# Second pair's Gram matrices ahead of the first merging, its inversion and solution inside the first pair's work, and a reordered opening

## The chip, the cores and the metric

The kernel runs on one core of a Trainium2 chip. The metric is the device time of one execution in microseconds; the time shown is the median of several executions. All times below come from these executions and from one profiled execution with its trace. The engines are TensorE (PE for its matmuls, PEld for its weight loads), VectorE (DVE), ScalarE (ACT), GpSimd (POOL) and SyncE (SP), which issues most DMAs.

## What is computed

For 32 sequences of 512 rows and 256 features: a delta-rule block with an MLP, both on normalized rows, then a gated MLP with integer weights, each added to its input.

```python
def delta(x, ...):
    q, k, v = jnp.split(x @ gates_w + gates_b, 3, axis=-1)
    lr = x @ lr_w + lr_b
    k = k / jnp.linalg.norm(k, axis=-1, keepdims=True)
    K = jnp.tril(jnp.einsum('ntc,nsc->nts', k, k), k=-1)
    u = solve_triangular(K + jnp.eye(T), v, lower=True)
    score = jnp.einsum('nsk,ntk->nst', q, k)
    y = jnp.einsum('nst,ntv->nsv', score, lr * u)
    return y @ out_w + out_b

def attn(x, ...):
    x = x + delta(layernorm(x, dn_g, dn_b), ...)
    return x + relu(layernorm(x, mn_g, mn_b) @ w1 + b1) @ w2 + b2

def ffn(x, ...):                     # wg, wu, wd = integers / 127
    return (silu(x @ wg.T) * (x @ wu.T)) @ wd.T

x = x + attn(_layernorm(x), ...)
x = x + ffn(_layernorm(x), ...)
```

## The kernel before

The 32 sequences are worked through in 16 pairs. A sequence is four chunks of 128 rows (NT = 4), its features two blocks of 128 (NF = 2). Everything is 32-bit float, and each product of 128 by 128 by some columns appears as two MATMUL records. The order of the work is written out by hand for every engine: each engine runs its instructions in program order, and the order of the Python calls is that order. Tiles come from rings of buffers by tag ("hid", "fz", "uv", "ps_a", "ps_f"), and a new tile waits for the last reader of the one whose place it takes.

A sequence goes through these steps:

- `normalized`: statistics on VectorE (L409, L410), centring with a sum on ScalarE (L527), scaling on VectorE (L543). `to_keys` turns it by TensorE for the first two pairs (tp_a, L465), later pairs by DMA (way_a, ag).
- `keys` (pk, L588) and `gram` (pg, L617): the Gram matrix in four block rows, copied by ScalarE into gd (diagonal blocks), go (blocks off the diagonal) and, in `give`, gs. `give` also sends the 32x32 diagonal blocks by eight DMAs a pair (given, L635) to DRAM.
- `invert` (L656 on): the blocks come back by one DMA (blocks, L661), and VectorE inverts the 128 small triangles of a pair in 15 steps of a product and a sum (xt, L710 and L716). The result goes out and back by DMA (found, yb, yfull). It is a generator that can run as a `Side`: `spend(cols)`, called after matmuls, lets it advance by so much weight per column. `norms` makes the factors kn.
- `solution`: `merge` joins the small inverses to 128x128 (xparts, pw, py, yfull; L750 to L798) in five steps, `solve` runs the block solution (pr, pu, rhs, dp) in eight more.
- values: `gather` (pf), `through_values` (pz), `through_keys` (pm), `answer` (po_d, then statistics m).
- first MLP (`middle`): `normed`, `turned`, `mlp_in` (pa), `mlp_out` (po_m), `residual`; then the gated MLP (`gated`, 84 steps, L1007) and its output `Down` (po_x, po_y), which runs beside the next pair's values.

In a regular pair the next pair's preparation, keys and Grams run within the gated MLP, its inversion within the values, and its merging and solution from `middle` into the gated MLP. In the first pair this starts up: gate weights are folded with the norm's gains (`Gates.fold`, wlast, wt, pbias), products lT and rv are made (`Gates.rest`), the first pair is inverted with nothing beside it but the second pair's keys and the turning of the integer weights (wd_t, wg_t, wu_t), and then merged and solved. The second pair's Grams stand between the first pair's values and answers (`first_values`), its inversion is a side of the first MLP and of the first gated MLP up to step BEGIN = 17, its merging begins after step 21.

Of the kernel before, what the change touches and what calls it, by code (L numbers as in the profile page):

```python
# [10 lines left out]
F32 = mybir.dt.float32  # L11
# [5 lines left out]
B = 32  # L17
# [5 lines left out]
def kernel(  # L23
# [46 lines left out]
    INVERT = 17 * 1024  # L70
    INVERT_FIRST = 15 * 1024

# [117 lines left out]
    nc.gpsimd.memset(sel[:, LAST:P], 1.0)  # L190

    class Gates:


        def __init__(self, gw):

            self.gw = gw
            self.gb = wk.tile([1, GC], F32, tag="feat", name="gb", bufs=4)
            self.wlast = wk.tile([P, GC], F32, tag="feat", name="wlast", bufs=4)
            self.wt = [wk.tile([P, GC], F32, tag="dp", name=f"wt{f}") for f in range(NF)]  # L200
            self.load(*CUTS[0], nc.scalar)
            self.dnb = by_feature(dn_b, "dnb", nc.sync)
            self.dng = by_feature(dn_g, "dng", nc.sync)
            self.glast = const.tile([P, 1], F32, name="glast")
            nc.sync.dma_start(self.glast, dn_g[C - 1 : C].partition_broadcast(P))
            self.put = wk.tile([P, NF, P], F32, tag="rhs", name="put", bufs=4)
            nc.gpsimd.memset(self.put, 0.0)
            nc.gpsimd.tensor_copy(self.put[:, :, LAST:P], self.dnb.unsqueeze(2))
# [18 lines left out]

        def fold(self, lo_, hi_):

            cut = slice(lo_, hi_)  # L230
            pb = ps_f.tile([P, 512], F32, tag="mm", name=f"pbias_{lo_}")
            pb = pb[:, : hi_ - lo_]
            for f in range(NF):
                nc.tensor.matmul(
                    pb, lhsT=self.put[:, f, :], rhs=self.gw[f][:, cut],
                    start=(f == 0), stop=False,
                )
            nc.tensor.matmul(pb, lhsT=sel, rhs=self.gb[:, cut], start=False, stop=True)
            nc.vector.tensor_scalar(
                self.wlast[:, cut], self.wlast[:, cut], self.glast, None, ALU.mult  # L240
            )
            for f in range(NF):
                nc.vector.scalar_tensor_tensor(
                    out=self.wt[f][:, cut], in0=self.gw[f][:, cut],
                    scalar=self.dng[:, f : f + 1], in1=self.wlast[:, cut],
                    op0=ALU.mult, op1=ALU.subtract,
                )
            nc.vector.tensor_tensor(
                self.wt[NF - 1][:, cut], self.wt[NF - 1][:, cut], pb, ALU.add
            )  # L250

        def keys(self):
            self.fold(*CUTS[0])
            for f in range(NF):
# [27 lines left out]

        def rest(self):
            nc.vector.tensor_scalar(obrow, self.obs, ident[:, LAST:P], None, ALU.mult)
            self.fold(*CUTS[1])
            self.fold(*CUTS[2])
            kT_ = self.turned(C, "wkT")
            qT_ = self.turned(0, "wqT")
            vT_ = self.turned(2 * C, "wvT")
            self.product(lT, kT_, qT_, "lT")  # L290
            self.product(rv, vT_, self.ow, "rv")

            ones = wk.tile([P, P], F32, tag="wl", name="ones", bufs=1)
# [10 lines left out]
            nc.scalar.copy(wl, pl)  # L304

        def load_rest(self):
            self.load(*CUTS[1], nc.sync)
            self.load(*CUTS[2], nc.sync)
            self.room = wk.tile([P, NH, NF, C], F32, tag="hid", name="room")
            self.rooms = 0  # L310
            self.ow = self.scratch("ow")
# [73 lines left out]
    class Combined:  # L385


        def __init__(self):
            self.b12 = wk.tile([P, NP, P], F32, tag="fz", name="b12", bufs=4)

# [191 lines left out]
    def keys(s, o):  # L582
        n = s.n
        if o == 0:
            s.kT = wk.tile([P, NF, T], F32, tag="ka", name=f"kT_{n}")
        pk = ps_a.tile([P, 512], F32, tag="mm", name=f"pk_{n}_{o}")
        for f in range(NF):
# [19 lines left out]
    def gram(s, j):  # L607
# [3 lines left out]
        if j == 0:  # L611
            s.gd = wk.tile([P, NT, P], F32, tag="gd", name=f"gd_{n}", bufs=2)
            s.go = {}
        w = (NT - j) * P
        pg = ps_a.tile([P, 512], F32, tag="mm", name=f"pg_{n}_{j}")
        for f in range(NF):
# [5 lines left out]
        if j < NT - 1:  # L622
            s.go[j] = wk.tile([P, w - P], F32, tag=f"go{j}", name=f"go_{n}_{j}", bufs=2)
            nc.scalar.copy(s.go[j], pg[:, P:w])
        spend(NF * w)

    def give(s, given):

        s.gs = wk.tile([P, NT, 2, B], F32, tag="gs", name=f"gs_{s.n}")
        second = s.gd.rearrange("p b (a h r) -> p b a h r", h=2, r=B)[:, :, :, 1, :]  # L630
# [26 lines left out]
    def invert(g, given, seqs):  # L657

        blocks = wk.tile([P, B, B], F32, tag="blocks", name=f"blocks_{g}", bufs=1)
        n, nq, ncol = len(seqs), columns.nq, columns.nc  # L660
        nc.sync.dma_start(  # L661
            blocks,
            given.rearrange("s b i e -> (s b i) e")[:, : B * B].unsqueeze(1).to_broadcast(
                [n * NT * NB, nq, B * B]
            ),
        )
        flat = blocks.rearrange("p i j -> p (i j)")
# [223 lines left out]

    def answer(s):
        pr = Project(ps_f, s.a, s.aT, s.m, NF, f"d{s.n}", s.r2[:, 0, :])
        s.norm = Norm(s.a, f"m{s.n}")
        for c in range(NT):
            pr.step(c)
            if c % 2 == 1:
                s.norm.measure(c - 1)
# [332 lines left out]

    whole = lambda gen: [None for _ in gen]

    def middle(old, rest, sides_, sol, following):
# [40 lines left out]
        if not rest:  # L1275
            next(sides_[0].gen)
            sides_[0].finish()

    def last_middle(old, rest):
        one, two = old  # L1280
# [20 lines left out]

    def first_values(seqs, following, norms_, inverse, given):

        one, two = seqs
        for _ in normalized(following[1]):
            pass
        gates.rest()
        for _ in inverse:
# [22 lines left out]
        for turn in turns[:2]:  # L1331
            for _ in turn:
                pass
        turns = turns[2]
        for s in seqs:
            for _ in rates(s):
                pass
        for _ in solution(seqs):
            next(turns, None)
        for _ in turns:  # L1340
            pass
        whole(gather(one))
        whole(gather(two))
        gram(following[0], 0)
        fetch_residual(one)
        biased(one)
        whole(through_values(one))
        gram(following[0], 1)
        fetch_residual(two)
        biased(two)  # L1350
        whole(through_values(two))
        gram(following[0], 2)
        whole(through_keys(one))
        gram(following[0], 3)
        give(following[0], given[0])
        answer(one)
        whole(through_keys(two))
        normed(one, "m")
        answer(two)
        gram(following[1], 0)  # L1360
        turned(one, "m")
        gram(following[1], 1)
        gram(following[1], 2)
        gram(following[1], 3)
        give(following[1], given[1])
        for s in following:
            for _ in rates(s):
                pass
        return sides_of(begun(following, given), INVERT_FIRST)

# [67 lines left out]
    with tc.manual_schedule(engines={  # L1438
# [5 lines left out]
        gw = [wk.tile([P, GC], F32, tag="a", name=f"gw{f}", bufs=6) for f in range(NF)]  # L1444
        size = NH * C
        places = [
            wk.tile([P, 2, size], I32, tag="hid", name="integers"),
# [9 lines left out]
        ]  # L1457
        load_a(first[0])
        gates = Gates(gw)
        load_a(first[1])  # L1460
# [9 lines left out]
        mnb = by_feature(mn_b, "mnb", nc.sync)  # L1470
        for _ in normalized(first[0]):
            pass
        to_keys(first[0])
        gates.keys()
        for _ in normalized(first[1]):
            pass
        given = new_given(0)
        for i, s in enumerate(first):
            if i:
                to_keys(s)  # L1480
                for _ in normalized(pairs[1][0]):
                    pass
            for o in range(NF):
                keys(s, o)
            in_order(s)
            grams(s)
            give(s, given[i])
        norms_, inverse = begun(first, given)
        for d, _ in quantized:
# [3 lines left out]
        for g in range(n_pairs):  # L1493
            new = pairs[g]
            following = pairs[g + 1] if g + 1 < n_pairs else None
            if not old:
                given = new_given(1)
                sides_ = first_values(new, following, norms_, inverse, given)
                rest = []
            else:  # L1500
                sol = solution(new)
                middle(old, rest, sides_, sol, following)
                prep = None
# [10 lines left out]
                for i, _ in enumerate(gated(old)):  # L1514
                    if i >= EARLY and i % 2 == 0 and solved:
                        next(early, lambda: None)()
                    if i == BEGIN and not rest:
                        sides_[1].finish()
                    if i % 3 == 2 and (rest or i >= BEGIN + 4):
                        solved = next(sol, sol) is sol  # L1520
# [72 lines left out]
```

## Time and profile before

| quantity | us |
|---|---|
| median of three executions (2070.45 to 2075.43) | 2072.32 |
| the profiled execution | 2069.12 |
| its span in the trace | 2067.3 |
| TensorE busy | 1992.1 (96%) |
| VectorE busy | 1370.9 (66%) |
| GpSimd busy | 1113.9 (54%) |
| ScalarE busy | 918.1 (44%) |
| first inversion on VectorE | 43.93 to 64.12 |
| first merging (pw) starts | 69.90 |
| first gather starts | 92.97 |
| second pair's inversion on VectorE | 134.09 to 166.7 |
| second merging (pw) starts | 172.15 |
| second pair's gather starts | 229.18 |

In lines of the trace the columns are: start and length in us, engine, line, operation, output and inputs by the program's names, shape, count, and in brackets the engine's idle time before it with what ended it. A granted clock (PEclk) of 1.00 is TensorE's full speed. A wait line reads: engine, waiting tile and line, what it waited for: us in total, times, longest.

### The profile page before, as it was taken

How to read it: one execution, taken by the hardware profiler on the slowest of the kernel's cores; microseconds unless marked ns; L12 is line 12 of the kernel's file. 1: busy time of each engine (PE TensorE's matmuls, PEld its weight loads, DVE VectorE, ACT ScalarE, POOL GpSimd, SP SyncE). 2: the span in 40 equal slices, each digit the busy share in tenths (PEclk: the TensorE clock that was granted, in tenths of full speed). 3: DMA queues.
4: the chain of work that ended last, by engine and by line, in shares of the span. 5: the costliest groups of instructions: out<-in, count | busy, mean ns of one | idle time of the engine just before them, and what ended most of it. 6: DMA issues, size and time to landing. Idle time of an engine off the chain costs nothing.

```text
span 2067.3 us, 31099 instructions
## 1 busy us (share of the span) xinstructions
PE 1992.1 (96%) x10286; PEld 1583.0 (77%) x10286; DVE 1370.9 (66%) x3788; ACT 918.1 (44%) x2499; POOL 1113.9 (54%) x1317
## 2 busy tenths in 40 slices
PE   6888999999999999999999999999999999999998
PEld 4657876878778687886878778687877878778887
DVE  5567584966848587584966848587585867848252
ACT  4235345353543535345353543535345353544443
POOL 3424464645546465454645536475455646536668
PEclk9899999999999999999999999999999999999999
DMA  5111242332323323142332323233242332423120
GB/s 146 28 34 29 53 132 58 90 99 60 105 63 100 83 71 112 50 134 57 90 102 61 106 62 100 83 76 107 58 126 64 94 90 61 113 54 100 42 62 21
DMA packets 248344, 164.12 MB, mean 79 GB/s; under 512 B 80849, under 2 KB 223832, under 8 KB 248184
## 3 DMA queue, kind: packets, MB, share of 16 engines
q1 hardware_dynamic: 247670, 161.61, 28.8%
q8 instruction: 82, 1.34, 0.3%
q14 instruction: 78, 0.64, 0.1%
q10 hardware_dynamic: 434, 0.39, 0.1%
q0 software_dynamic: 80, 0.14, 0.0%
HBM read 96.02 MB, written 66.06 MB: 78 GB/s over the span
## 4 chain that ended last, share of the span: by engine, by line
PE 72%; DVE 16%; DMA 6%; ACT 2%; issue 2%; POOL 1%; SPq 1%; POOLq 0%; DVEq 0%; ACTq 0%
PE po_y L1134 6%; PE pg L617 6%; PE pyup L1007 5%; PE pk L588 5%; PE pygate L1007 5%; PE pa L951 5%; PE po_m L876 5%; PE po_d L876 4%; PE pr L814 4%; PE po_x L1134 4%; PE pzup L1007 4%; PE pf L835 4%; PE pzgate L1007 4%; DMA ag<-way_a 3%; PE pu L824 3%
## 5 line engine op out<-in xcount | busy, mean ns | idle before, releaser
L1047 POOL TENSOR_TENSOR v_up<-v_up,five_up 128x256 f32<-128x256 f32 x96 | 70.0, 729 | 266.5 <-ACT v_up L1021 266.5
L1070 DVE TENSOR_TENSOR top_up<-top_up,pzup 128x512 f32<-128x512 f32 x96 | 65.5, 682 | 218.2 <-PE pzup L1007 215.7
L1134 PEld LDWEIGHTS po_y<-wdS,hid 128*128 128x128 f32 x1536 | 179.7, 192 | 4.1 <-issue 1.0
L1134 PE MATMUL po_y<-wdS,hid 128*128 128x128 f32 x1536 | 182.8, 276 | 0.0
L1007 PE MATMUL pygate<-hS,wgS 128*128 128x256 f32 x576 | 175.0, 386 | 4.6 <-ACT top_gate L1041 2.3
L1007 PE MATMUL pyup<-hS,wuS 128*128 128x256 f32 x576 | 174.5, 385 | 1.9
L617 PE MATMUL pg<-kT 128*128 128x256 f32 (+3 forms) x512 | 157.6, 433 | 1.9 <-ACT kT L595 1.9
L1134 PEld LDWEIGHTS po_x<-wdS,hid 128*128 128x128 f32 x1152 | 138.4, 192 | 5.1 <-POOL hid L1071 1.9
L1134 PE MATMUL po_x<-wdS,hid 128*128 128x128 f32 x1152 | 138.9, 275 | 1.7 <-POOL hid L1071 1.7
L1053 POOL TENSOR_TENSOR hid<-v_gate,five_gate 128x256 f32<-128x256 f32 x96 | 69.7, 726 | 130.7 <-ACT v_gate L1021 130.7
L1075 DVE TENSOR_TENSOR hid<-top_gate,pzgate 128x512 f32<-128x512 f32 x96 | 65.1, 678 | 112.4 <-PE pzgate L1007 112.4
L1007 PEld LDWEIGHTS pyup<-hS,wuS 128*128 128x128 f32 x576 | 106.2, 190 | 43.1 <-issue 13.4
L1007 PEld LDWEIGHTS pygate<-hS,wgS 128*128 128x128 f32 x576 | 106.4, 190 | 41.7 <-issue 12.4
L588 PE MATMUL pk<-ag,wa 128*128 128x512 f32 x256 | 122.5, 603 | 13.6 <-DMA ag<-way_a 12.5
L1048 POOL TENSOR_TENSOR hid<-hid,v_up 128x256 f32<-128x256 f32 x96 | 70.3, 733 | 102.9 <-ACT hid L1054 93.1
L876 PE MATMUL po_m<-w2s,act 128*128 128x256 f32 x512 | 125.4, 389 | 0.1
L1071 POOL TENSOR_TENSOR hid<-hid,top_up 128x512 f32<-128x512 f32 x96 | 122.4, 1275 | 0.3 <-DVE bnst_a L409 0.3
L617 PEld LDWEIGHTS pg<-kT 128*128 128x128 f32 x512 | 92.0, 190 | 37.1 <-issue 9.3
L1007 PE MATMUL pzup<-hT_f,wuS 128*128 128x256 f32 x384 | 117.9, 389 | 1.2 <-ACT five_up L1021 0.7
L951 PE MATMUL pa<-hT_m,w1s 128*128 128x512 f32 x256 | 116.7, 598 | 1.9 <-DMA hT_m<-way_m 1.9
L835 PE MATMUL pf<-a,dp 128*128 128x256 f32 x512 | 115.4, 379 | 0.0
L1007 PE MATMUL pzgate<-hT_f,wgS 128*128 128x256 f32 x384 | 115.2, 382 | 0.1
(242 smaller groups left out, 4905.4 us busy)
## 6 DMA issues: line engine op xcount, KB each, us to landing
a<-in_L_attn_x_dram SPq DMA_DIRECT2D x32, 512.0 KB, 4.7
x<-in_L_attn_x_dram SPq DMA_DIRECT2D x32, 512.0 KB, 4.3
out_dram<-a SPq DMA_DIRECT2D x64, 256.0 KB, 2.8
way_m<-turn_m SPq DMA_DIRECT2D x120, 128.0 KB, 2.4
hT_m<-way_m SPq DMA_DIRECT2D x30, 512.0 KB, 4.0
way_a<-turn_a SPq DMA_DIRECT2D x112, 128.0 KB, 2.3
ag<-way_a SPq DMA_DIRECT2D x28, 512.0 KB, 3.6
way_f<-turn_f SPq DMA_DIRECT2D x112, 128.0 KB, 2.3
```

The costliest lines, as they stand in the source:

```text
L588: nc.tensor.matmul(pk, lhsT=wa[:, f, ts(o, P)], rhs=s.ag[:, f, :], start=(f == 0), stop=(f == NF - 1),)
L617: nc.tensor.matmul(pg[:, :w], lhsT=s.kT[:, f, ts(j, P)], rhs=s.kT[:, f, j * P :], start=(f == 0), stop=(f == NF - 1),)
L814: nc.tensor.matmul(pr, lhsT=s.go[j][:, ts(i - j - 1, P)], rhs=p_[:, j, :], start=(j == 0), stop=(j == i - 1),)
L835: nc.tensor.matmul(s.pp[:, o, :], lhsT=lhs[:, c, ts(o, P)], rhs=rhs[:, c, :], start=(c == 0), stop=(c == nk - 1),)
L876: nc.tensor.matmul(self.po[:, c % 2, :], lhsT=src[:, ts(c, P)], rhs=self.w[:, f, :], start=(f == 0), stop=(f == self.nk - 1),)
L951: nc.tensor.matmul(pa, lhsT=w1s[:, f, ts(o, P)], rhs=s.hT[:, f, :], start=(f == 0), stop=(f == NF - 1),)
L1007: nc.tensor.matmul(dst, lhsT=self.w[:, self.j, self.SLOT[i], :], rhs=self.s.B[i], start=first, stop=last, skip_group_check=True,)
L1047: nc.gpsimd.tensor_tensor(v, v, self.five, ALU.add)
L1048: later(5, lambda: nc.gpsimd.tensor_tensor(self.out(1, 1), self.out(1, 1), self.half(v), ALU.mult))
L1053: nc.gpsimd.tensor_tensor(to, self.half(v), self.half(self.five), ALU.add)
L1071: later(4, lambda: nc.gpsimd.tensor_tensor(natural(g), natural(g), grouped(flat(self.top)), ALU.mult))
L1134: nc.tensor.matmul(po[:, i, :], lhsT=self.A[block][:, j, :], rhs=wdS[:, j, slot, :], start=(j == 0), stop=(j == NP - 1),)
```

## The change

Five things are done. The gains of the gate weights are split from `fold` and made earlier (`gains`), `bias` and `shift` stay; the preparation of the later sequences is cut into pieces between keys and Grams. The first pair's blocks are loaded in two halves, one a sequence. The second pair's keys and Grams use ps_f, and the Grams of both sequences lie in one tile of tag "hid", filled ahead of the first merging. Its inversion becomes a side of the first pair's values (weight spread over 17 x 1024 columns instead of 15 x 1024). A `first_middle` takes its merging in, and the first gated MLP goes on with the solution from its third step.

```diff
-    INVERT_FIRST = 15 * 1024
+    INVERT_FIRST = 17 * 1024
...
-        def keys(self):
-            self.fold(*CUTS[0])
+        def shift(self, to, pb):
+            nc.vector.tensor_tensor(to, to, pb, ALU.add)
+
+        def keys(self, between):
+            folded = self.fold(*CUTS[0])
+            between()
+            self.shift(*folded)
...
-        def rest(self):
-            nc.vector.tensor_scalar(obrow, self.obs, ident[:, LAST:P], None, ALU.mult)
-            self.fold(*CUTS[1])
-            self.fold(*CUTS[2])
+        def rest(self, prep):
+            for folded in [self.bias(*cut) for cut in CUTS[1:]]:
+                self.shift(*folded)
...
+            whole(prep)
...
+        def gains(self):
+            for cut in CUTS[1:]:
+                self.gain(*cut)
+            nc.vector.tensor_scalar(obrow, self.obs, ident[:, LAST:P], None, ALU.mult)
...
-            self.b12 = wk.tile([P, NP, P], F32, tag="fz", name="b12", bufs=4)
+            self.b12 = wk.tile([P, NP, P], F32, tag="uv", name="b12", bufs=1)
...
-        pk = ps_a.tile([P, 512], F32, tag="mm", name=f"pk_{n}_{o}")
+        pk = (ps_f if n // NS == 1 else ps_a).tile([P, 512], F32, tag="mm", name=f"pk_{n}_{o}")
...
+            if n // NS == 1:
+
+                if n % NS == 0:
+                    pairs[1][1].some = s.some = wk.tile(
+                        [P, NS, NT * (NT + 3) // 2 * P - T // 2], F32, tag="hid", name="grams",
+                    )
...
+        parts = n if g == 0 else 1
+        for q in range(parts):
+            rows = slice(q * (n // parts), (q + 1) * (n // parts))
+            nc.sync.dma_start(
+                blocks[q * (P // parts) : (q + 1) * (P // parts)],
...
+    def first_middle(old, newer, sides_, sol, following):
+        one, two = old
+        step = lambda: next(sol, None)
+        normed(two, "m")
+        mlp_in(one, 0)
+        mlp_in(one, 1)
+        turned(two, "m")
+        sides_[1].finish()
+        next(sides_[0].gen)
+        sides_[0].finish()
+        residual(one)
+        for s in newer:
+            whole(rates(s))
+        mlp_out(one, 0)
+        mlp_out(one, 1)
+        residual(two)
+        mlp_in(two, 0)
+        step()
+        mlp_in(two, 1)
+        normed(one, "f")
+        step()
+        mlp_out(two, 0, step)
+        turned(one, "f")
+        step()
+        whole(mixed(one))
+        mlp_out(two, 1, step)
+        load_a(following[0])
...
+        for s, m in zip(following, given):
+            grams(s)
+            give(s, m)
+        gens = begun(following, given)
         for s in seqs:
-            for _ in rates(s):
-                pass
+            whole(rates(s))
         for _ in solution(seqs):
-            next(turns, None)
+            next(turns[2], None)
+        whole(turns[2])
+        sides_ = sides_of(gens, INVERT_FIRST)
+        next(gens[1])
         whole(gather(one))
-        whole(gather(two))
-        gram(following[0], 0)
+        other = gather(two)
+        next(other)
         fetch_residual(one)
         biased(one)
         whole(through_values(one))
+        whole(other)
+        whole(through_keys(one))
         fetch_residual(two)
         biased(two)
         whole(through_values(two))
-        gram(following[0], 2)
...
+        answer(one, lambda: whole(through_keys(two)))
         normed(one, "m")
         answer(two)
-        gram(following[1], 0)
         turned(one, "m")
...
+        prep = normalized(first[1])
+        gates.keys(lambda: some(prep, NT - 1))
+        some(prep, 2)
         given = new_given(0)
+        some(prep, 2)
+        keys(first[0], 0)
+        some(prep, 1)
+        keys(first[0], 1)
+        some(prep, 1)
+        in_order(first[0])
+        grams(first[0])
+        give(first[0], given[0])
+        inverse = invert(first[0].n, given, first)
+        next(inverse)
+        whole(prep)
+        to_keys(first[1])
+        prep = normalized(pairs[1][0])
+        some(prep, NT + 3)
+        gates.gains()
+        last = normalized(pairs[1][1])
+        some(last, NT + 1)
+        keys(first[1], 0)
...
-                    if i == BEGIN and not rest:
-                        sides_[1].finish()
-                    if i % 3 == 2 and (rest or i >= BEGIN + 4):
+                    if i % 3 == 2:
                         solved = next(sol, sol) is sol
```

## The prediction

> **What bounds the kernel now.** I read first the page's 40 slices, then a cut of the span into stages at the points that the change touches, then TensorE's waits up to 230 us, then TensorE and VectorE in order of time through those stages.
>
> ```profile
> PE   6888999999999999999999999999999999999998
> PEclk9899999999999999999999999999999999999999
> ```
>
> From the sixth slice on TensorE is full at full clock. A change to the opening can only win in the first five slices, and can only lose where it disturbs the rest. The stages (columns: start:end, length, busy us and instructions of PE, PEld, DVE, ACT, POOL, granted clock, DMA share, GB/s) are: opening up to the first merging, merging and solving of the first pair, its values, its first MLP with the second pair's inversion, its gated MLP with the second pair's solution, one regular pair, all others.
>
> ```profile
> 10.99:69.90 58.91, 47.94 (x182) 29.30 (x182) 44.33 (x147) 28.09 (x89) 26.38 (x19) 0.93 0.38 102
> 69.90:92.97 23.07, 21.73 (x112) 16.98 (x113) 9.79 (x21) 4.47 (x14) 5.69 (x9) 0.65 0.00 1
> 92.97:124.45 31.48, 30.95 (x137) 24.37 (x136) 11.72 (x48) 9.86 (x26) 7.96 (x10) 1.00 0.14 36
> 124.45:150.26 25.81, 19.97 (x67) 12.49 (x65) 16.27 (x49) 10.39 (x24) 5.84 (x7) 0.88 0.24 65
> 150.26:229.18 78.92, 70.96 (x330) 54.29 (x328) 46.35 (x125) 40.39 (x115) 29.64 (x36) 0.95 0.13 33
> 229.18:354.72 125.54, 122.23 (x634) 96.79 (x633) 84.18 (x227) 56.29 (x157) 65.83 (x79) 1.00 0.32 85
> ```
>
> TensorE idles 58.91-47.94 = 10.97, then 1.34, 0.53, 5.84 and 7.96 us: 26.6 us. The missing clock is worth 0.07x58.91 + 0.35x23.07 + 0.12x25.81 + 0.05x78.92 = 4.1+8.1+3.1+3.9 = 19.2 us. So 46 us is the ceiling. Who ended the waits:
>
> ```profile
> PE pw L756 <- DVE xparts L751: 7.8, 2, 4.5
> PE tp_f L465 <- ACT turn_f L446: 4.5, 1, 4.5
> PE pygate L1007 <- ACT top_gate L1041: 2.3, 1, 2.3
> PE pwqT L267 <- DVE wt L243: 2.3, 1, 2.3
> PE pg L617 <- ACT kT L595: 1.9, 1, 1.9
> PE pygate L1007 <- DVE hid L1075: 1.2, 1, 1.2
> ```
>
> Both mergings wait for the inversion behind xparts (4.50 and 3.29 us), and after each such gap the clock is halved. The same sixteen pw take 1.97 us at 69.90 and 1.15 in the next pair:
>
> ```profile
> 69.90 1.97 PE L756 MATMUL pw<-xparts,gs 128*64 128x64 f32 x16 [4.50 <-DVE xparts L751]
> 271.33 1.15 PE L756 MATMUL pw<-xparts,gs 128*64 128x64 f32 x16
> ```
>
> **The change part by part**, stage by stage against the profiled execution's own times.
>
> **Opening (58.91).** ScalarE's four centrings (x8, 2.07 us) no longer stand as a block ahead of the two kT copies: of pg's 1.91 us and the later overlaps I take 2.05. The gains (0.35+0.88 for one cut, 0.35+0.89 for the other, obrow 0.35: 2.8 us of VectorE) and the last sequence's statistics (some 2.5) move into VectorE's waits of 4.03 us at 29.4 and 3.66 at 37.8. The folds then end with their bias matmuls, and the waits 2.30+0.53+0.45 = 3.28 before pwqT and pwvT go; with them the half clock of 42 to 48 us (pwqT, plT 3.62 against 1.89 for eight matmuls of the same shape, prv) is worth 2.5. The second pair's 32 Gram matmuls come here: 1.72+1.29+0.86+0.43 = 4.3 us a sequence, 8.6 for both; they stand where the 4.50 wait was. VectorE then decides: spread ends near 39.3, the inversion (43.93 to 64.12, 20.2 us) starts there, ends at 59.9, and b1s, w1s (2.2), eight rates (2.75) and two transposes (0.9) bring the first pw to 65.75; TensorE, by its own rows, reaches it at 65.4. The blocks must be there by 39.5: the second half's load now waits only for the second sequence's givens; the split adds one DMA of about 0.6 us on SP, which is waiting for givens anyway, and without that cover costs 0.6. So the opening takes 54.8: **-4.1** net of the 8.6.
>
> The bound: if VectorE's order is worse by the whole 2.05, 0; if the block load is the limit (38.44 issue to 43.93 at most in the trace, only 1.4 us earlier now), 2.8 later.
>
> **Merging and solving (23.07).** No work changes; the clock does. pw, py, pw, py took 1.97, 1.92, 1.97, 1.94 against 1.15, 1.12, 1.14, 1.14: 3.25; two pu blocks 2.07+1.82 against 1.03 each: 1.83; pr 1.91 against 1.03: 0.88. **-5.9**. TensorE would be some 74% busy in the merging; the slices of 2 us with 1.28 and then 0.41 busy (152 to 156) kept clock 1.00, so I let it stay.
>
> **Values (31.48).** The Gram matrices leave (8.7 with their overlaps) and an m wait of 0.46: 22.3. Here the inversion comes in, with its blocks and ss DMAs ahead of the x loads on SP (SP is free near 71, the x loads are due near 86). 17,408 columns for its weight let its 15 steps run through to the last answer. VectorE gets 20.2 us of inversion and 8.5 of answers (four halves of 0.88+0.74+0.30, two m of 0.42) beside 20.8 us of TensorE, and is late. Placed step by step, the first answer's statistics end some 22.35 us after the stage's start, r_m and mr_m (1.04+0.20 and gaps) at 23.7, ScalarE's chunks 24.3 to 25.8; TensorE is ready for tp_m at 20.8. A new wait of 3.5 us plus a paced tp_m, 4.3 together: 26.6, **-4.9**.
>
> **First MLP (25.81).** Gone: 0.90+0.16 before tp_m, 4.51 before tp_f, 3.0 of half clock. In: four merging blocks of 1.08 (4.3), and two waits for ScalarE, whose turn_m of the second sequence now stands ahead of the relus and waits for statistics that end behind the inversion's last step (28.95): 1.4+0.9 = 2.3. And the clock: a 3.5 us gap is like the 3.29 and 4.50 that were followed by half speed; 3 us (the half clock priced in this stage now), counted at 0.8: 2.4. Sum -8.6+9.0, say **0**. If VectorE keeps up, 9 us better; if its lag is double, about 6.6 more wait here and in the values, and with another cold stretch (3) 10 worse.
>
> The yb round trip (xc copied at 166.66, transposed at 171.21) hides behind mlp_out of the first sequence. The rates (2.75 us of VectorE) stand after residual in the first MLP; the first sequence's output waits for them, inside the 2.3.
>
> **Gated MLP (78.92).** Merging leaves (-4.3), the waits 3.29, 1.24, 0.69, 0.34 go, 1.3 of the 2.31 goes (turn_f of the second sequence is less late), half clock at 172 to 178 (pw 0.82, pzup, pygate, pyup 1.6, py 0.5) -3.0; a wait of 1.2 for ag, as at 326.88 in the next pair, comes. **-12.9**. The solution ends near step 26 of 84; the second hid takes the Gram tile's place and is first written past step 42, 16 steps or 7 us later. Without that cover the hid copies would wait for the last pr.
>
> The smaller buffers (b12 in uv, keys and Grams in four ps_f banks instead of ps_a's three) cost nothing: ScalarE empties a Gram in 0.75 us while the first two take 1.72 and 1.29.
>
> **Sum:** -4.1-5.9-4.9+0-12.9 = -27.8. Own time 2069.12 (span 2067.3 and 1.8 around it) gives 2041.3; the median 2072.32 lies 3.2 above, and I predict **2044** for the median.
>
> **Rivals.**
>
> *VectorE becomes the bound of the values and the first MLP.* For it: between gather and the gated MLP VectorE has 20.2+8.5, residuals 2.4, rates 2.75, four halves of mlp_out 6.6 and some 3 of merging, 43 us, against 44 of TensorE. Against: only tp_m, m and mlp_out wait for it. Price 10 over mine: about 2054.
>
> *VectorE keeps up.* For it: steady pairs run inversion and values together with waits of 0.7 (po_d on m). Against: they have Down work beside it. 9 us better: 2035.
>
> *The two sequences' Grams in one tile are held as one.* Then ScalarE's copies for the second wait until the first's given DMAs, behind found, yb and yfull on SP (near 66), have read it: Grams finish near 72, 6 late, 3 of clock: 2053. Against: pg starts at 30.50 while the second half of kT is copied until 31.3, so parts of a tile are separate.
>
> [...]
>
> *Slower.* One mechanism: the rotation of the hid buffers (room, integers, Grams, then the sequences) leaves a later hid waiting for its old reader, in each of 15 remaining pairs. It decides above 27.8/15 = 1.9 us a pair; at 2.5 it gives 2072.3-27.8+37.5 = 2082. Against: Down's po_y ends long before the next gated MLP, and no row shows such a wait.
>
> **How the numbers follow.** Forecast 0.50 (own range 2038 to 2050), VectorE bound 0.25, VectorE keeping up 0.13, one tile 0.05, transposes 0.03, slower 0.04. The range 2034 to 2057 leaves out the slower case and the outer halves of others. 0.2% is 4 us, about what can be told from no change: faster 0.94, same 0.02, slower 0.04.
>
> **What would show it.** Right: first pw near 66 with no gap over 2 us and pw, py near 1.15; gather near 83; tp_m waiting some 3 us for turn_m; the second gather near 201; a regular pair still 125.5. Wrong: po_d waiting for m, clock under 0.9 from 66 to 83, or regular pairs that changed.

## The result, and the profile after

The changed kernel takes 2045.57 us in the median of four executions (2041.05 to 2049.42), the kernel before 2072.47 on the same chip (2070.45 to 2075.43): a ratio of 0.9868 with a 95% interval of 0.9843 to 0.9893, 26.9 us less. The profiled execution took 2047.26 us, with a span of 2045.2 us against 2067.3 before.

The 40 slices of the changed kernel (tenths busy, tenths of full clock):

```profile
PE   7999999999999999999999999999999999999998
PEclk9899999999999999999999999999999999999999
```

TensorE's first four slices read 6888 before and 7999 now; the clock still has its 8 in the second. The same stages as before, cut at the same points (the last row at the same length) (columns: start:end, length, busy us and instructions of PE, PEld, DVE, ACT, POOL, granted clock, DMA share, GB/s): opening; merging and solving of the first pair; values; first MLP; gated MLP; one regular pair.

```profile
11.16:70.30 59.14, 55.48 (x214) 33.79 (x215) 44.20 (x147) 32.58 (x105) 27.93 (x22) 1.00 0.38 99
70.30:92.55 22.25, 20.89 (x113) 16.14 (x114) 9.78 (x21) 4.47 (x14) 4.27 (x5) 0.69 0.13 29
92.55:118.79 26.24, 22.64 (x106) 19.00 (x104) 24.44 (x68) 5.81 (x12) 6.28 (x6) 1.00 0.13 41
118.79:142.00 23.21, 22.30 (x128) 15.13 (x128) 17.41 (x54) 10.47 (x23) 8.56 (x14) 0.93 0.24 63
142.00:206.52 64.52, 62.82 (x267) 48.41 (x266) 33.83 (x86) 39.89 (x115) 25.94 (x31) 1.00 0.13 34
206.52:332.06 125.54, 122.51 (x637) 97.44 (x636) 87.06 (x241) 56.52 (x155) 68.50 (x82) 1.00 0.32 85
```

| stage | before | after | difference | forecast |
|---|---|---|---|---|
| start of TensorE | 10.99 | 11.16 | +0.2 | 0 |
| opening | 58.91 | 59.14 | +0.2 | -4.1 |
| merging and solving | 23.07 | 22.25 | -0.8 | -5.9 |
| values | 31.48 | 26.24 | -5.2 | -4.9 |
| first MLP | 25.81 | 23.21 | -2.6 | 0 |
| gated MLP | 78.92 | 64.52 | -14.4 | -12.9 |
| from the second gather to the end | 1838.1 | 1838.7 | +0.6 | 0 |
| span | 2067.3 | 2045.2 | -22.1 | -27.8 |

Read the third and the fifth row against those of before. TensorE's busy time fell from 30.95 to 22.64 us in the values and from 70.96 to 62.82 in the gated MLP: the Gram matrices and the second merging have left, and with them some half speed in the gated MLP. The opening took up the Grams (PE 47.94 to 55.48 busy) at no length. The merging is still at a clock of 0.69. TensorE's waits up to 205 us (what waited, for what: total us, times, longest):

```profile
PE tp_a L483 <- DVE a L561: 11.2, 1, 11.2
PE tp_m L483 <- ACT turn_m L464: 3.4, 4, 2.9
PE pw L799 <- DVE xparts L794: 2.4, 1, 2.4
PE pk L606 <- ACT ag L485: 0.9, 3, 0.4
PE pzup L1052 <- ACT five_up L1066: 0.9, 2, 0.6
```

Of the waits for xparts (7.8 in two) 2.4 is left; the waits for turn_f and top_gate (4.5 and 2.3) are gone; a wait of tp_m for turn_m is new, as the prediction had it. In order of time on TensorE (start, length, line, operation, output and inputs, shape, count, and in brackets the idle time before it):

```profile
16.39 5.34 PE L606 MATMUL pk<-ag,wa 128*128 128x512 f32 x8
...
58.52 8.90 PE L648 MATMUL pg<-kT 128*128 128x512 f32 x32
...
70.30 1.48 PE L799 MATMUL pw<-xparts,gs 128*64 128x64 f32 x16 [2.44 <-DVE xparts L794]
72.76 1.92 PE L811 MATMUL py<-yb,wparts 128*64 128x32 f32 x16
...
116.31 0.33 PE L483 MATMUL tp_m<-ident,turn_m 128*128 128x128 f32 x1 [2.88 <-ACT turn_m L464]
...
118.79 5.34 PE L996 MATMUL pa<-hT_m,w1s 128*128 128x512 f32 x8 [0.24 <-ACT hT_m L487]
...
132.55 1.12 PE L799 MATMUL pw<-xparts,grams 128*64 128x64 f32 x16 [0.64 <-POOL r_f L433]
```

Both waits are followed by half speed: py takes 1.92 us, the eight pa 5.34 (3.70 at full clock, in a run below). The second merging, inside the MLP, starts after 0.64 us and runs at full clock (pw 1.12 us). Why the opening isn't shorter stands on VectorE and in SP's queue:

```profile
41.10 0.48 DVE L313 TENSOR_SCALAR spread<-ident,wt 128x128 f32<-128x128 f32 x2
43.41 0.36 DVE L717 RECIPROCAL few<-blocks 128x32 f32<-128x32 f32 x1 [1.83 <-DMA blocks<-given]
```

```profile
35.84 2.47 SPq L672 DMA_DIRECT2D given<-gd  x4
39.48 0.54 SPq L702 DMA_DIRECT2D blocks<-given  x1
```

The inversion begins at 43.41, after 1.83 us in which VectorE had nothing but the blocks to wait for. Their load is issued at 39.48, behind the landing of the givens, and lands 3.9 us later. Before, it was issued at 38.44 and VectorE, busy with the folds, came to it at 43.93.

### The profile page after: what moved, and what is told of

Its sections match the earlier page's. It is cut to its first block, busy times and chain, and to the rows that moved or that the text cites. A ratio compares the mean times of both kernels' runs of the same rounds, so it can differ in the third digit from the quotient of the medians.

```text
span 2045.2 us, 31109 instructions
## 1 busy us (share of the span) xinstructions
PE 1984.0 (97%) x10286; PEld 1578.3 (77%) x10286; DVE 1374.9 (67%) x3788; ACT 919.1 (45%) x2499; POOL 1114.7 (55%) x1317
## 4 chain that ended last, share of the span: by engine, by line
PE 71%; DVE 17%; DMA 6%; issue 2%; ACT 1%; POOL 1%; SPq 1%; POOLq 0%; ACTq 0%; DVEq 0%
PE po_y L1179 6%; PE pg L648 6%; PE po_m L919 5%; PE pa L996 5%; PE pk L606 5%; PE pyup L1052 5%; PE pygate L1052 5%; PE pr L857 4%; PE po_d L919 4%; PE po_x L1179 4%; PE pzup L1052 4%; PE pf L878 4%; PE pzgate L1052 3%; DMA ag<-way_a 3%; PE pu L867 3%
```

## The experiments

Each run stands beside runs of the kernel before on the same chip (medians 2072.68 to 2075.29); the ratios are to those. Four questions were put: what the reordered opening is worth, why the clock still falls, what VectorE sets behind it, and how far one execution differs from another. In the diffs, ... marks lines that are left out.

**The changed kernel again.** Nothing is edited.

> The changed kernel unaltered, beside the others on the same chip, to have its spread and another profile: median 2043 to 2048; the second gather near 203 to 207 depending on how long the half clock lasts at the start and in the merging, in steps of 3.4 us.

Measured: median 2047.19 (2042.84 to 2047.90), ratio 0.9866 [0.985, 0.9883]. Its stages lie within 0.8 us of those above. With the first set, eight executions lie between 2041.05 and 2049.42, so a difference below some 4 us of two medians is not read as one here.

**The opening alone**, on the kernel before: gains and preparation cut into pieces, blocks in two loads; the Grams, inversion and merging of the second pair stay.

```diff
-        gates.keys()
...
+        prep = normalized(first[1])
+        gates.keys(lambda: some(prep, NT - 1))
...
+        inverse = invert(first[0].n, given, first)
+        next(inverse)
...
+        gates.gains()
```

> The kernel before with the new opening alone (gains early, preparation in pieces, blocks in two halves); Grams, inversion and solution of the second pair stay where they were. Theory A (the block load and the inversion set the first merging): first pw within 1 us of 69.9, TensorE idles some 10 us ahead of it, the whole within 2 us of before. Theory B (TensorE's order sets it, as the forecast had it in part): first pw near 61, the whole about 8 us faster than before.

Measured: median 2074.60 of ten (2066.66 to 2078.20), ratio 1.000 [0.9986, 1.0014]. The first merging starts at 68.98 instead of 69.90. TensorE's first pw in its profile:

```profile
68.98 1.97 PE L780 MATMUL pw<-xparts,gs 128*64 128x64 f32 x16 [8.01 <-DVE xparts L775]
```

The wait has grown from 4.50 to 8.01 us: what the order saves TensorE, it waits for. In the median the opening by itself is worth nothing; without the moved Grams there is no work to put into the time. But the ten executions fall into two groups: seven take 2074.28 to 2078.20 at a mean granted clock of 0.987 to 0.991, three take 2066.66 to 2067.98 at 0.994 to 0.995. The profile is of one of the seven (2076.20); what the three kept at full clock no profile shows.

**The changed kernel with the opening of before**, three kernels of the same text, of which one was profiled without further timing.

```diff
-        prep = normalized(first[1])
-        gates.keys(lambda: some(prep, NT - 1))
...
+        gates.keys(lambda: None)
+        whole(normalized(first[1]))
...
-        parts = n if g == 0 else 1
+        parts = 1
```

> The changed kernel with the old opening (preparations as blocks, gains with the folds, blocks in one load); Grams ahead of the first merging, inversion in the values and first_middle stay. Theory A (gap sets clock): TensorE reaches the first pw late, near 74, without a gap, the merging runs at full clock in 17 us, first gather near 91.5: as fast as the changed kernel or 1 us faster. Theory B (merging always at half clock): pw near 74, gather near 96.5, 4 us slower than the changed kernel.

> The changed kernel with the old opening once more, for another profile: its four times were 2047.5 and three of 2054.5 to 2056.6, and the profile was of the fastest. Theory A (the phase of the clock's stretches decides, some 3.4 us each): a time near 2054 shows two or more further stretches at half clock before 130 us, and regular pairs as always. Theory B (regular pairs vary): the first 210 us as in the first profile, and the rest 7 us longer.

> The changed kernel with the old opening a third time, timed in five rounds: its two profiles gave 2047.5 and 2048.1 us, equal to the changed kernel's 2047.3 and 2047.9, its three unprofiled times 2054.5 to 2056.6. Theory A (the new opening is worth nothing while the clock falls in the merging after it): median 2046 to 2049. Theory B (the unprofiled times stand for it, and the new opening is worth some 8 us once the Grams stand ahead of the merging): median 2053 to 2057.

Measured: medians 2054.56 (2047.47 to 2056.58), ratio 0.9915 [0.9899, 0.9932], and 2051.60 (2048.47 to 2055.21), ratio 0.9898 [0.9882, 0.9914]; the single one 2048.07. All ten together have a median of 2052.5, against 2047.1 for the eight of the changed kernel. The first pw comes later (73.84, 73.82 and 75.68 instead of 70.30 and, in the repetition, 70.88), but without a gap, and the merging is 19.2 to 19.5 long instead of 22.2, so that the second gather is at 207.43, 207.81 and 209.16 against 206.52 and 207.79.

The rest lies in single executions, not in a stage. Two profiles of the same text are of executions of 2047.47 and 2053.38 us. Of these 5.9, 1.7 lie ahead of the second gather, where the slower one has 3.4 us more at half speed from 22.2 on and 6.8 instead of 3.4 from 42.6 on. 4.2 lie behind it, and two regular pairs make them up, with 126.07 and 125.65 us instead of 123.79 and 123.27. In each of these two pairs, pk waits for its input and 3.4 us at half speed follow. The first such pk, and the same one in the changed kernel, where nothing follows:

```profile
926.88 3.57 PE L606 MATMUL pk<-ag,wa 128*128 128x512 f32 x4 [1.88 <-DMA ag<-way_a]
```

```profile
925.22 1.98 PE L606 MATMUL pk<-ag,wa 128*128 128x512 f32 x4 [2.05 <-DMA ag<-way_a]
```

So regular pairs do vary from one execution to the next, and the clock is a part of it. Whether the opening of before makes such executions more frequent, as the medians suggest, stays open; the single execution of 2048.07 looks like the faster of the two.

What the first of these runs shows of the clock: there is no wait before pw, pw and py run at full clock, and yet it falls, at 81.2 us, still within the merging, in a wait of 0.95 us for yfull:

```profile
80.00:82.00 2.00, 1.05 (x14) 0.92 (x12) 1.58 (x2) 0.00 (x0) 2.00 (x3) 0.80 0.16 1
82.00:84.00 2.00, 2.00 (x6) 1.37 (x5) 0.48 (x1) 0.59 (x2) 1.70 (x2) 0.50 0.00 0
```

The first of these slices has 1.05 us of work, the next one is full, at half clock.

**The blocks in one load.**

```diff
-        parts = n if g == 0 else 1
+        parts = 1
...
-        next(inverse)
```

> The changed kernel with the first pair's blocks in one load after both sequences' givens, as before, instead of two halves. Theory A (the load's size and its place behind the givens set the inversion's start at 43.4): the load lands 1 to 2 us later, the first inversion starts near 45, the first pw near 72, the whole 1 to 2 us slower than the changed kernel. Theory B (the split buys nothing, since the second half lands with the traffic of the integer loads anyway): reciprocal within 0.5 us of 43.4, no change.

**The integer loads ahead of everything**, so that they don't run beside the blocks.

```diff
+        for d, _ in quantized:
+            d.load()
...
-        for d, _ in quantized:
-            d.load()
```

> The changed kernel with the integer weights' loads (2.25 MB) issued right after the small constants, ahead of the givens on SP, in the slices of 22 to 36 us where the DMA engines are nearly idle, instead of behind ss, where they fill the engines from 41 to 50. Theory A (that traffic slows the second half of the blocks, 3.9 us to landing): it lands in 2.5 us or less, the inversion starts when VectorE is ready near 41.6 to 42, pw 1.4 to 1.8 us earlier relative to the first transposes. Theory B (the landing time is the load's own, or the givens come later behind the integers): start within 0.5 us of 43.4, no change.

Measured: 2047.25 (2045.65 to 2049.78), ratio 0.9866 [0.9845, 0.9886], and 2050.03 (2045.45 to 2054.86), ratio 0.9878 [0.9855, 0.9902]. Neither is told from the changed kernel. The inversion starts at 41.16 and 40.83, openings 57.08 and 56.60. That is 2 us shorter than above, but so it is in three more profiles in which neither was touched (41.58, 41.69, 40.90), and it isn't in two others (43.73, 43.76). What goes with it is the start of TensorE:

| profile | first eight pk start, take | inversion starts |
|---|---|---|
| changed kernel | 16.39, 5.34 | 43.41 |
| the same again | 16.20, 5.77 | 43.73 |
| blocks in one load | 15.39, 3.86 | 41.16 |
| integers early | 15.51, 3.86 | 40.83 |

The first matmuls run slowly for longer in one execution than in another, and the whole opening follows. Neither the split nor the traffic sets the blocks. In all these profiles the inversion waits for them, by 1.6 to 2.3 us.

**Full products ahead of the first merging**: three products of 128 by 128 by 512, whose result nobody reads, in the wait for xparts.

```diff
+        fill = ps_f.tile([P, 512], F32, tag="mm", name="fill")
+        for _ in range(3):
+            nc.tensor.matmul(
+                fill, lhsT=wa[:, 0, 0:P], rhs=following[1].ag[:, 0, :], start=True, stop=True
+            )
         for _ in solution(seqs):
```

> The changed kernel with three more 128x512 products, whose result nobody reads, placed on TensorE between the second pair's Grams and the first merging, where it idled for 2.44 us. Theory A (the gap alone drops the clock): no gap over 0.5 us before the first pw, clock 1.00 from 66 to 83, pw and py at 1.1 to 1.2 us, merging and solving 17 us instead of 22.25, the whole about 5 us faster than the changed kernel. Theory B (the merging itself keeps TensorE too idle for full clock): clock falls within the merging, the stage stays near 22, the whole within 1 us of the changed kernel.

Measured: median 2041.20 (2040.14 to 2044.21), ratio 0.985 [0.9835, 0.9865]. TensorE in its merging:

```profile
68.39 1.15 PE L799 MATMUL pw<-xparts,gs 128*64 128x64 f32 x16
...
72.12 1.14 PE L821 MATMUL pw<-xparts,gd 64*64 64x64 f32 x16 [0.16 <-DVE xparts L815]
...
74.16 1.94 PE L837 MATMUL py<-yfull,wl 64*64 64x64 f32 x16 [0.47 <-ACT wuS L394]
```

The wait is gone and three of the four blocks run at full clock, then it falls at 73.5 all the same. The stage takes 20.11 us instead of 22.25: the gap was a cause, but not the only one.

**Products between the steps of the merging, too**: 256, 128, 256 and 512 columns of the same kind.

```diff
+        sizes = iter([0, 256, 128, 256, 512])
         for _ in solution(seqs):
             next(turns[2], None)
+            cols = next(sizes, 0)
+            if cols:
+                nc.tensor.matmul(
+                    fill[:, :cols], lhsT=wa[:, 0, 0:P], rhs=following[1].ag[:, 0, :cols],
...
```

> The changed kernel with the three unread products ahead of the first merging, and four more between the merging's steps (256, 128, 256 and 512 columns), where TensorE waits for VectorE. In the runs so far the clock fell 3 to 8 us after the first pw even where no gap stood ahead of it, while the merging's rows showed TensorE 88% busy. Theory A (TensorE's waits and small products in the merging drop the clock): with full-size products in between, clock stays 1.00 from 66 to 90, merging and solving take 17.5 to 18.5 us instead of 20.1, the whole 6 to 8 us below the changed kernel. Theory B (not the use of TensorE but something else drops it, as VectorE's or the DMAs' activity): clock falls again, the stage takes 20 us or more, the added products cost their 1 us.

Measured: median 2041.05 (2040.65 to 2043.22), ratio 0.9846 [0.9831, 0.986]. The merging and solving in its profile:

```profile
67.87:86.20 18.33, 17.86 (x122) 13.10 (x122) 10.07 (x20) 5.12 (x16) 4.31 (x5) 1.00 0.16 36
```

A clock of 1.00 for the first time, and 18.33 us: 4.7 less than before the change, with more work. This run both closes the short waits and adds large products; which of the two holds the clock it doesn't tell. In the median it can't be told from the one before; in its profiled execution two regular pairs have 3.4 us each at half speed (from 297.6 and from 546.8), which the one before has not; their mean granted clocks are 0.996 and 0.997.

**Three more, ahead of tp_m**, for the second stretch of half clock.

```diff
         answer(two)
+        fill = ps_a.tile([P, 512], F32, tag="mm", name="fill_m")
+        for _ in range(3):
+            nc.tensor.matmul(
...
```

> As the kernel with seven unread products in and before the merging, and three more of 512 columns after the first pair's answers, in the wait of 2.88+0.5 us before tp_m is done. Theory A: no half clock at 114 to 118, pa takes 3.6 us instead of 5.3 and the first MLP 1.7 us less. Theory B (the first MLP is set by VectorE's lag, so that a faster pa waits for turn_m of the second sequence): pa is faster but the first MLP stays at 23.2 us within 0.5.

Measured: median 2039.32 (2037.04 to 2043.28), ratio 0.9837 [0.9823, 0.9852]. The first pa and the whole first MLP:

```profile
115.56 3.70 PE L996 MATMUL pa<-hT_m,w1s 128*128 128x512 f32 x8 [0.24 <-ACT hT_m L487]
```

```profile
115.56:138.77 23.21, 21.66 (x128) 14.50 (x129) 17.41 (x54) 10.47 (x23) 8.56 (x14) 1.00 0.25 63
```

The clock is 1.00 and pa is 1.64 us shorter, but the stage is 23.21 us as before, and the gated MLP is 65.88 instead of 64.52. So TensorE's speed doesn't set this stage. Behind the faster pa the transposes of the second sequence wait for its turn_m (0.5 us in three pieces), which in the changed kernel was ready by then; the statistics for it stand on VectorE behind the inversion's last step. Values, first MLP and gated MLP together take 113.97 in the changed kernel, 114.89 without and 115.34 with these three products, so they bring nothing.

**The second inversion spread thinner**, so that the answers and their statistics come between its steps.

```diff
-    INVERT_FIRST = 17 * 1024
+    INVERT_FIRST = 26 * 1024
```

> The changed kernel with the second pair's inversion spread over 26 x 1024 columns instead of 17 x 1024, so that its last third comes after the first pair's answers on VectorE. Theory A (the inversion's steps on VectorE delay the answers' statistics): the wait before tp_m falls from 2.88+0.5 to under 1 us, turn_m of the second sequence comes some 5 us earlier, the whole 2 to 4 us faster. Theory B (what is saved there comes back before the second merging, since xparts then wait for yb): tp_m waits less but pw waits 3 us or more, the whole within 1 us.

Measured: median 2048.29 (2046.22 to 2053.00), ratio 0.9885 [0.9866, 0.9904]. Its TensorE:

```profile
113.48 0.33 PE L483 MATMUL tp_m<-ident,turn_m 128*128 128x128 f32 x1 [2.31 <-ACT turn_m L464]
...
132.20 1.12 PE L799 MATMUL pw<-xparts,grams 128*64 128x64 f32 x16 [2.33 <-POOL r_f L433]
```

The wait for turn_m falls from 2.88 to 2.31, the one ahead of the second merging grows from 0.64 to 2.33. Values and first MLP take 25.82+25.55 = 51.4 instead of 49.5. The weight only moves the wait. That the amount of VectorE's work sets the two stages is not shown by it: VectorE is busy for 41.96 us in them, 41.85 in the changed kernel, and of the 1.9 us more some belong to the clock, which is at half speed for 6.8 us instead of 3.4 (the first eight pa take 6.00 us).

**Fillers and early integer loads together.** All products of the run with three groups, and the loads ahead.

```diff
+        for d, _ in quantized:
+            d.load()
...
+            cols = next(sizes, 0)
...
+        fill = ps_a.tile([P, 512], F32, tag="mm", name="fill_m")
```

> The kernel with ten unread products (before the first merging, within it and before tp_m) together with the early integer loads. If both effects hold they add: first pw 57 to 58 us after the first transposes with the long start at half clock, merging and solving 18.3, first MLP with no half clock, median 2037 to 2039, against 2039.3 without the early loads and 2045 to 2047 for the changed kernel. If only the clock matters, the median stays at 2039 to 2041.

Measured: median 2038.49 of five (2037.26 to 2040.28), ratio 0.9824 [0.9805, 0.9844]; all five lie below the fastest of the changed kernel's eight. Opening, merging and values of its profile:

```profile
11.14:68.00 56.86, 55.64 (x220) 33.92 (x221) 44.23 (x147) 31.92 (x103) 27.88 (x22) 1.00 0.37 104
68.00:86.32 18.32, 17.86 (x121) 13.10 (x121) 10.06 (x20) 5.12 (x16) 4.31 (x5) 1.00 0.17 37
86.32:112.56 26.24, 25.21 (x111) 20.13 (x109) 24.44 (x68) 5.80 (x12) 6.28 (x6) 1.00 0.13 40
```

It beats both kernels: the one before by 36.8 us (2075.29 on the same chip), the changed one by 7.1 to 8.7. From the run with fillers alone (2039.32) it can't be told, so the early loads have no part that is shown. Of its gain over the changed kernel 3.9 us are the merging; some 2 are the short start of this execution; its rest behind the second gather is 1835.1 us against 1838.7, which no step explains; the clock is full in both there until the last 1.4 us.

## Why the prediction was right, step by step

The forecast, 2044 with faster by far the likeliest, came true within 1.6 us. But its own time for the profiled execution was 2041.3, and that took 2047.26. The sum of the steps was 5.7 us too hopeful, and the median hid this: before, it lay 3.2 above the profiled execution, now it lies 1.7 below. That the number came so close is partly luck; within the sum, errors of +4.3 and +5.1 stand against -2.6 and -1.5.

- **Opening, -4.1; measured +0.2.** The mis-sized term is the start of the inversion: 39.3 was forecast, 43.41 came. (Its end was put at 59.9; 39.3 and the 20.2 that it takes make 59.5.) Two things make the 4.1. The slow start was longer in this execution than in the profile before: the bias products and pk took 1.91+1.22+5.34 against 1.54+0.69+3.87, 2.4 more, which ate the 2.05 taken for pg's wait and the overlaps. In the executions with a short start VectorE is done with the folds at 39.2 to 39.6, as forecast, but the inversion begins at 40.8 to 41.7, and the opening takes some 57, so about -1.9 is its like-for-like size. The rest, about 2, is the blocks' chain: from the end of the second sequence's pg (35.34, where the next matmul starts) it is 8.1 us to the first reciprocal, through the givens' issue (to 38.31), their landing, the load at 39.48 and 3.9 more. That was the named bound, "if the block load is the limit", and it is the limit, whether the load is split or not. That VectorE decides the end of the opening and that the Grams fit into the wait was right: 8.6 us of them cost nothing.
- **Merging and solving, -5.9; measured -0.8.** The step that failed is "so I let it stay". The clock fell to half from 70.9 to 84.6 us. The prediction listed a clock under 0.9 from 66 to 83 as what would prove it wrong, and it was 0.64. It leaned on two slack slices (1.28 and 0.41 us busy of 2, a wait of 2.31) that had kept the full clock. Behind a wait of 2.44 us ahead of the merging it didn't stay, and elsewhere two waits of one length, 2.31 us, ended differently (last section). And with that wait filled the clock falls all the same, later, in the merging's own steps. With fillers the stage is 18.33, 4.7 less than before, so the prices of the blocks were nearly right and only their condition was missing.
- **Values, -4.9; measured -5.2.** Right by its parts: tp_m's first wait 2.88 and 3.4 in all, 3.5 forecast; the Grams' 8.7 us gone.
- **First MLP, 0; measured -2.6.** What was off is that 2.3 for waits on ScalarE and 2.4 for the clock were added; of the 4.7 some 1.7 came (25.81-8.6+4.3 = 21.5, and 23.21 was measured). The half clock came, for 3.4 us from 118.7, but cost nothing: with full clock the stage has the same 23.21 us. TensorE's slow pa stood in time that it would have waited; in the run with three groups of fillers what it waits for there is turn_m of the second sequence.
- **Gated MLP, -12.9; measured -14.4.** The wait of 1.2 for ag didn't come, all of top_gate's 2.3 went instead of 1.3, of the wait for hid (1.24) 0.7 stayed, and 0.9 came for five_up, whose 0.69 was to go: -1.2-1.0+0.7+0.9 = -0.6. The other 0.8 is busy time, 70.96-62.82 = 8.1 less, where 7.3 was priced for merging and clock.
- **Regular pairs, 0; measured +0.6** over 1838 us. From the second gather to the third it is 124.80 us, 125.54 before. No hid waited for an old reader, so the slower rival has nothing in the trace.

Of the other rivals, VectorE as the bound is half true: TensorE waits for turn_m at the end of the values and, at full clock, in the first MLP, but at the price already in the forecast, not at 10 us more. VectorE keeping up fell with the wait of tp_m. Grams held as one tile: pg of the second pair's two sequences ran as one row of 32 matmuls in 8.90 us, so nothing waited between them. For the chance of 0.03 on transposes no run shows anything: wd_t and wg_t stand right ahead of the same row (54.56 to 58.41), and it took 8.90 us for the 8.6 priced at full clock.

## What to carry to other kernels

When work is moved into the wait of another step, look at what the clock does behind the rest of that wait: a term "full speed again" held in the first merging only where TensorE was kept full through the step (17.86 of 18.33 us busy, clock 1.00; 0.69 in the changed kernel, 0.83 with only the wait ahead of it filled), and the seven products that did it, which nobody reads, cost nothing in the median (2041.05 us). That the clock stayed full behind a wait elsewhere is no evidence for another of the same length: behind two waits of 2.31 us it was 1.00 and 0.50. Speed on an engine that waits anyway was worth nothing here (pa 1.64 us shorter, the first MLP 23.21 us as before): price a clock or a shorter instruction in a stage only after asking which engine ends that stage. And compare a stage of a start-up between two executions only if their first matmuls took the same time (eight pk of 5.34 and 3.86 us went with inversions from 43.41 and 41.16).

## What the runs showed of the hardware

The clock fell after short waits, of 1.88 to 2.44 us in the second table below. Granted clocks in slices of half a microsecond give these stretches at half speed between 40 and 215 us:

| kernel | half speed (us) | length |
|---|---|---|
| before | 41.6-48.4, 68.9-85.9, 144.0-150.8, 171.3-178.1 | 6.8, 17.1, 6.8, 6.8 |
| after | 70.9-84.6, 118.7-122.1 | 13.7, 3.4 |
| the same again | 71.6-85.3, 116.0-122.8 | 13.7, 6.8 |
| fill ahead of the merging | 73.4-80.3, 114.4-117.8 | 6.8, 3.4 |
| fill in the merging | 109.8-116.7 | 6.8 |
| all three fills, and with early loads | none | |
| opening alone | 64.6-85.1, 143.2-150.0, 170.5-177.3 | 20.5, 6.8, 6.8 |

The lengths are multiples of some 3.41 us: a single stretch takes 3.40 to 3.42 (fill ahead of the merging, from 114.4; the slower profile of the opening of before, from 83.6 and from 121.1), a double one 6.83 (fill ahead of the merging, from 73.4; fill in the merging).

The starts, too, lie multiples of 3.41 us apart within one profile. Before the change the distances are 27.30, 75.10 and 27.30 us, that is 8, 22 and 8 times 3.41; after it 47.8, 14 times; with the fill ahead of the merging 41.0, 12 times; in the slower profile of the opening of before 37.5, 11 times. So the stretches of each of these profiles lie on a grid of 3.41 us, and it lies differently against the work in the next execution: the second stretch of the changed kernel starts 0.1 us ahead of the first pa, that of its repetition 3.4 us ahead. Laid through the starts of each profile, pieces of 3.41 us held this:

| profile, piece (us) | what TensorE waited for in it | TensorE busy | clock in the next piece |
|---|---|---|---|
| before, 150.80-154.21 | 0.93 of the 2.31 for top_gate | 73% | 1.00 |
| before, 154.21-157.62 | the other 1.38 | 60% | 1.00 |
| after, 67.51-70.92 | all 2.44 ahead of pw | 28% | 0.50 |
| thinner spread, 110.54-113.95 | all 2.31 ahead of tp_m | 28% | 0.50 |
| thinner spread, 127.61-131.02 | 1.15 of the 2.33 ahead of the second pw | 67% | 1.00 |
| thinner spread, 131.02-134.43 | the other 1.18 | 65% | 1.00 |
| opening of before, slower profile, 923.28-926.69 | 1.69 of the 1.88 for ag | 49% | 0.50 |
| after, 924.25-927.67 | 0.97 of the 2.05 for ag | 71% | 1.00 |
| after, 111.88-115.29 | 1.86 of the 2.88 ahead of tp_m | 45% | 1.00 |
| after, 115.29-118.71 | the other 1.02, then transposes | 51% | 0.50 |
| fill ahead, 70.03-73.44 | small products of the merging, no wait over 0.35 | 85% | 0.50 |

Two waits of 2.31 us, one split between two pieces and one inside one, had opposite ends, a clock of 1.00 and of 0.50. So the length of a wait alone doesn't tell; neither does the busy share alone, by the last three rows (45% ahead of 1.00, 51% and 85% ahead of 0.50). What else decides stays open. Waits of 1.88 to 2.44 us that lay almost whole in one piece (1.69 of 1.88, all of 2.31 and of 2.44) were followed by half speed in the next; one of 2.88, with 1.86 in one piece, was not.

How it ends, in slices of the changed kernel:

```profile
72.00:74.00 2.00, 2.00 (x16) 1.67 (x15) 0.65 (x2) 0.65 (x2) 0.00 (x0) 0.50 0.20 32
74.00:76.00 2.00, 2.00 (x16) 1.60 (x16) 0.44 (x1) 0.72 (x2) 0.00 (x0) 0.50 0.23 39
...
82.00:84.00 2.00, 2.00 (x7) 1.20 (x5) 1.10 (x3) 0.74 (x2) 0.47 (x1) 0.50 0.00 0
84.00:86.00 2.00, 1.97 (x8) 1.19 (x7) 1.17 (x3) 0.49 (x2) 0.00 (x0) 0.86 0.00 0
```

TensorE is shown busy for all of 72 to 76 with sixteen matmuls a slice, the merging's products of 32 and 64 columns and a few transposes, and stays at half speed; the full clock is back at 84.6, in the solution's 128 by 128 by 256 products, which run from 80.79. So 4.00 us shown busy of 4 did not bring the clock back here; whether it is the size of the products, or pauses between them that the rows don't show, no run separates.

At the start the granted clock of the changed kernel reads 1.00 (11 to 23 us), and yet eight tp_a take 2.45 us where the eight tp_m at 123.97 take 1.04, and eight pk 5.34, in other executions 3.86 to 6.02: so a first slow stretch isn't in that column, and its length changes from one execution to the next.
